# ScalarE copies and GpSimd sums in the post-attention chain, and expert tiles loaded six ahead

## The chip, the cores and the metric

The kernel runs on one core of a Trainium2 chip. A core has five engines that run their own instruction streams: TensorE (PE in the profile, with its weight loads as PEld), VectorE (DVE), ScalarE (ACT), GpSimd (POOL) and SyncE (SP, which here only issues DMA transfers). Matrix products land in PSUM, a small memory of eight banks of 128 partitions by 512 float32 numbers; everything else is kept in SBUF. The metric is device microseconds from the start to the end of one execution of the program; lower is better.

## The reference

The input x has 2 sequences of 2048 tokens with 256 features. All is float32, and every layernorm uses eps 1e-5.

1. Attention with 16 heads of 16 features: `qkv = x @ qkv_w + qkv_b`, a rotation of q and k (its angle depends on the head), scores divided by 4, softmax over all 2048 keys, the sum of values, `@ out_w + out_b`.
2. `x = layernorm(x + attention)`.
3. `n = layernorm(x) * g1 + be1`, then `x2 = x + n + n @ mix_w + mix_b`.
4. A mixture of 8 experts on `n2 = layernorm(x2) * g2 + be2`: router probabilities `softmax(n2 @ router_w)`, the best two experts of each token with those probabilities as weights (not normalised again), each expert `silu(n2 @ w1 + b1) @ w2 + b2` with 1024 hidden features, the weighted sum added to x2.
5. `out = layernorm(x + that)`, where x is the result of step 2.

## The kernel before, in words

**Attention.** The work is cut into 8 blocks of 512 query rows (4 per sequence). For each block there are four visits, one per group of four heads, so 32 visits in all; a visit walks over the 2048 keys in 16 chunks of 128. One chunk of one visit is a step, and there are 512 steps. A step of visit w does this:

- scores of 4 heads (L545), corrected by the row maxima through a second small product (L554), into four PSUM banks; ScalarE turns each into exponentials (L560, four instructions of 128x512);
- the value product of the step before (L575), which accumulates the unnormalised output in one PSUM bank; the values carry a column of ones, so that the sum of exponentials comes out as one more row;
- row maxima for a later visit, 18 steps ahead: four products (L501), two at a time, each into a bank of its own, and VectorE's maximum over each (L509, four reduces of 128x512). When a visit's maxima are complete, VectorE makes them ready (L519, L525, L528).

PSUM has three banks (`ps_mx`) for the row-maxima products and for everything that is done on the side. Two of them take the products of a half step; `bank(...)` takes one for each extra.

**The chain of a block.** Work on the side is entered by `later(k, f)`, to be done k steps later, and is handed out between the pieces of the steps, in an order that the program writes out by hand for TensorE, ScalarE, VectorE and SyncE. GpSimd's order is left to a scheduler. After a visit's last step ScalarE copies its output out of PSUM (L590). One step later `divide` transposes it (L597), VectorE takes the reciprocal of the sums (L600) and multiplies (L601) into `otok`. With a block's third group the input rows are fetched and GpSimd adds a bias row to them (`residual`, L660). With its fourth group the chain starts: `block` transposes the output (ScalarE empties the bank, L623), then `project` multiplies by `out_w`, in two halves of 256 rows. `two_products` does one half: eight matmuls into one bank (L636) and VectorE's addition to the residual (L643), then the moments of two groups of 128 rows, one per step (L647, L648). `norms` takes the layernorm's factors (L707, L708, and the square root by Newton steps in L137 to L146), with ScalarE and GpSimd applying them (L716, L730, L727). The second product, `mix`, uses `two_products` again. `lists` then takes another layernorm (L772), `logits` the router's product, `choose` the best two experts (L849 to L874), `places` the position of each row in its expert's list (L891 to L908), and GpSimd scatters the rows into the lists in HBM (L912).

The chain of a block runs during the next block's visits, one chain at a time. A block lasts 64 steps. The last two blocks of the 8 have a shorter time to finish in: the last one has its own pace (`pitch`, `gap`) and VectorE in place of GpSimd for the small operations. The projections to q, k and v of the second sequence are also done on the side, during the first blocks.

**Experts.** The lists are cut into 46 tiles, 25 whole ones of 256 rows and 21 half ones of 128. Each tile loads its rows (`xg`, L1239), the expert's `w1` and `w2` (1 MB each, L1252 and L1253), and its biases, all on SyncE's queue. Before, the loads are entered four tiles ahead: tiles 0 and 1 have their own two weight buffers in one pool, the others share four in another. TensorE transposes a tile's rows (L1269, emptied by VectorE, L1273), does the hidden product (L1298, then silu on ScalarE, L1307), and, one tile later, the second product (L1315). VectorE adds the bias and multiplies by the router's weight (L1325, L1326); GpSimd issues a DMA that adds the rows to `acc` in HBM (L1327, the scatter). These scatters, 71 in all, run in order.

**The end.** `acc` is read back in 8 parts, and each part is normalised (L1376 to L1385) and stored.

The functions that the change touches, and what calls them:

Of the kernel before, what the change touches and what calls it, by code (L numbers as in the profile page):

```python
# [32 lines left out]
P = 128  # L33
# [30 lines left out]
def seq_postln_kernel(  # L64
# [88 lines left out]
    with ExitStack() as actx:  # L153
# [431 lines left out]
        def attn_out(w):  # L585

            b, qb, g = visits[w]
            av = av_of.pop(w)
            avs = bp.tile([P, 512], F32, name="avs", tag="avs", bufs=2)
            nc.scalar.copy(avs, av)  # L590
            if g == 0:
                otok[b, qb] = bp.tile([P, 4, D], F32, name=f"otok_{b}_{qb}", tag="otok", bufs=1)

            def divide():
                ps = bank("ps_o", 4, P)
                for i in range(4):
                    nc.tensor.transpose(ps[:, i, :], avs[:, i * P : (i + 1) * P], ident)  # L597
                psv = ps.rearrange("p i (h c) -> p i h c", c=32)
                rd = bp.tile([P, 4, 4], F32, name="rd", tag="rd", bufs=2)
                nc.vector.reciprocal(rd, psv[:, :, :, HD])  # L600
                nc.vector.tensor_tensor(  # L601
                    otok[b, qb][:, :, g * 64 : (g + 1) * 64].rearrange(
                        "p i (h d) -> p i h d", d=HD
                    ),
                    psv[:, :, :, 0:HD],
                    rd.unsqueeze(3).to_broadcast([P, 4, 4, HD]),
                    ALU.mult,
                )
                if g == G - 2:
                    residual(b, qb)  # L610
                if g == G - 1:
                    later(1, lambda: holding("chain", block, b, qb))

            later(1, divide, 0.5, urgent=True)
# [15 lines left out]
        def two_products(name, turned_in, w, k, sum_, mv):  # L630
# [12 lines left out]
            nc.vector.tensor_add(sum_[:, 2 * k : 2 * k + 2, :], sum_[:, 2 * k : 2 * k + 2, :], ps)  # L643
# [6 lines left out]
            for i in range(2):  # L650
                later(1 + i, lambda i=i: moments(2 * k + i))
# [12 lines left out]
        def block(b, qb):  # L664
# [22 lines left out]
            def project(k):  # L687
                two_products("ps_p", oT, ow, k, xr, mv)
                if k == 1:
                    later(3, lambda: norms(n, xr, mv, eng, pitch, gap))  # L690
# [4 lines left out]
        def norms(n, xr, mv, eng, pitch, gap):  # L695
# [61 lines left out]
            def mix(k):  # L757

                two_products("ps_mix", nT, mixw, k, x2, mv2)
                if k == 1:  # L760
                    later(3, lambda: lists(n, xr, x2, mv2, eng, gap))
# [459 lines left out]
    first_tile = (0, NEARLY, NWHOLE)  # L1221

    def load_tile(t):
# [8 lines left out]
        pool, bufs = (wtp, 2) if t < 2 else (kp, 4)  # L1232
        b1 = kp.tile([P, NFC], F32, name=f"b1_{t}", tag="b1", bufs=5) if t >= 2 else wtp.tile(
            [P, NFC], F32, name=f"b1_{t}", tag="b1", bufs=2
        )
        w1t = pool.tile([P, 2, F], F32, name=f"w1_{t}", tag="w1", bufs=bufs)
        w2t = pool.tile([P, NFC, D], F32, name=f"w2_{t}", tag="w2", bufs=bufs)
        xg = wtp.tile([P, ns, D + 2], F32, name=f"xg_{t}", tag="xg", bufs=6)
# [16 lines left out]
        def load_b2():  # L1255
            b2t = kp.tile([P, D], F32, name=f"b2_{t}", tag="b2", bufs=6)
            nc.sync.dma_start(out=b2t, in_=b2[bass.ds(e, 1)].to_broadcast([P, D]))
            return b2t
# [78 lines left out]
    with tc.manual_schedule(engines=IN_ORDER):  # L1337
        DEPTH = 4
# [21 lines left out]
    for n in range(NTB):  # L1360

        o = (
            kp.tile([P, 4, D], F32, name=f"o_{n}", tag="o", bufs=NTB - 2)
            if n >= 2
            else wtp.tile([P, 2, F], F32, name=f"o_{n}", tag="w1", bufs=2)[:, 0, :].rearrange(
                "p (i d) -> p i d", i=4
            )
        )
        nc.sync.dma_start(out=o, in_=of[n])  # L1369
        os_.append(o)  # L1370
# [102 lines left out]
```

## Time and profile before

| | us |
|---|---|
| median of 3 runs | 2277.39 |
| lowest and highest of them | 2276.5, 2279.97 |
| the profiled execution | 2287.95 |
| its span | 2286.2 |
| busy: TensorE | 2209.9 (97%) |
| busy: VectorE | 1540.7 (67%) |
| busy: ScalarE | 1368.0 (60%) |
| busy: GpSimd | 471.3 (21%) |
| L509, row maxima on VectorE, 2048 reduces | 1274.2 |
| L560, exponentials on ScalarE, 2048 | 1057.6 |

The median is taken over runs without a profile, and the profiled execution is a run of its own, 10.56 us above it. All views of the trace are of that execution, and times in them count from the start of its span. A group row reads: line, engine, operation, written tile <- read tiles, shapes, how many, then busy time and the mean duration of one in ns, then the idle time of the engine just before them and what ended it. A timeline row reads: start and duration in us, engine, line, operation; in brackets the idle time before it and what ended that. A busy TensorE is not TensorE at its peak: a matmul that is held in the pipeline counts as busy. The granted clock of TensorE in this execution was 0.991 of full speed.

### The profile page before, as it was taken

How to read it: one execution, taken by the hardware profiler on the slowest of the kernel's cores; microseconds unless marked ns; L12 is line 12 of the kernel's file. 1: busy time of each engine (PE TensorE's matmuls, PEld its weight loads, DVE VectorE, ACT ScalarE, POOL GpSimd, SP SyncE). 2: the span in 40 equal slices, each digit the busy share in tenths (PEclk: the TensorE clock that was granted, in tenths of full speed). 3: DMA queues.
4: the chain of work that ended last, by engine and by line, in shares of the span. 5: the costliest groups of instructions: out<-in, count | busy, mean ns of one | idle time of the engine just before them, and what ended most of it. 6: DMA issues, size and time to landing. Idle time of an engine off the chain costs nothing. (4 is left out here: it accounts for less than half of the span.)

```text
span 2286.2 us, 39759 instructions
## 1 busy us (share of the span) xinstructions
PE 2209.9 (97%) x14192; PEld 1319.6 (58%) x14192; DVE 1540.7 (67%) x3108; ACT 1368.0 (60%) x2724; POOL 471.3 (21%) x826
## 2 busy tenths in 40 slices
PE   9999999999999999999999999999999999999992
PEld 4444555545555555555555555545548888889982
DVE  7887788788878888888888888888825211112213
ACT  2577667677767776677777667777774222222323
POOL 3112201231131112021111202112122322222113
PEclk9999999999999999999999999999999999999996
DMA  7635322221131111221111222111036677668995
GB/s 237 209 111 159 123 83 87 99 96 56 56 130 66 47 65 66 80 79 49 64 47 65 67 81 76 47 66 56 10 117 207 194 203 200 195 194 241 294 310 191
DMA packets 176117, 275.64 MB, mean 121 GB/s; under 512 B 22000, under 2 KB 107760, under 8 KB 175920
## 3 DMA queue, kind: packets, MB, share of 16 engines
q1 hardware_dynamic: 154960, 231.69, 30.8%
q0 software_dynamic: 20544, 40.59, 6.8%
q8 instruction: 112, 1.84, 0.3%
q14 instruction: 85, 0.70, 0.1%
q10 hardware_dynamic: 416, 0.83, 0.1%
HBM read 211.89 MB, written 62.74 MB: 120 GB/s over the span
## 5 line engine op out<-in xcount | busy, mean ns | idle before, releaser
L509 DVE TENSOR_REDUCE pm<-ps_mx 128x1 f32<-128x512 f32 x2048 | 1274.2, 683 | 191.1 <-PE ps_mx L501 181.9
L560 ACT ACTIVATE ex<-ps_sc 128x512 f32<-128x512 f32 x2048 | 1057.6, 603 | 355.2 <-PE ps_sc L554 332.8
L501 PE MATMUL ps_mx<-km,qm 64*128 64x512 f32 x2048 | 566.7, 469 | 19.3 <-DVE pm L509 17.9
L575 PE MATMUL av<-ex,vt 128*32 128x512 f32 x4096 | 546.2, 605 | 0.0
L501 PEld LDWEIGHTS ps_mx<-km,qm 64*128 64x128 f32 x2048 | 282.0, 183 | 452.3 <-DVE pm L509 340.3
L545 PE MATMUL ps_sc<-qm,km 64*128 64x512 f32 x2048 | 421.8, 394 | 0.0
L554 PE MATMUL ps_sc<-mrow,sel 64*128 64x512 f32 x2048 | 419.8, 393 | 0.7 <-ACT mrow L535 0.5
L1307 ACT ACTIVATE hT<-ps_h,b 128x256 f32<-128x256 f32 (+1 forms) x368 | 143.4, 426 | 365.4 <-PE ps_h L1298 277.3
L1298 PE MATMUL ps_h<-xT,w 128*128 128x256 f32 (+1 forms) x1472 | 258.5, 332 | 4.8 <-ACT hT L1307 2.7
L1315 PE MATMUL ps_y<-w,hT 128*128 128x256 f32 x1136 | 253.9, 379 | 2.1 <-DVE y L1325 2.1
L1298 PEld LDWEIGHTS ps_h<-xT,w 128*128 128x128 f32 x1472 | 222.0, 190 | 36.9 <-ACT hT L1307 7.9
L554 PEld LDWEIGHTS ps_sc<-mrow,sel 64*128 64x128 f32 x2048 | 204.2, 184 | 52.5 <-ACT mrow L535 9.6
L1315 PEld LDWEIGHTS ps_y<-w,hT 128*128 128x128 f32 x1136 | 212.0, 190 | 29.3 <-DVE y L1325 2.5
L545 PEld LDWEIGHTS ps_sc<-qm,km 64*128 64x128 f32 x2048 | 204.6, 185 | 37.2 <-ACT ex L560 15.4
L1273 DVE TENSOR_SCALAR xT<-ps_x,cols_sb 128x256 f32<-128x256 f32 (+1 forms) x92 | 40.1, 478 | 236.1 <-PE ps_x L1269 233.1
L1327 POOL DMA_INDIRECT acc<-y,xg x71 | 110.3, 1553 | 368.7 <-DVE y L1326 148.5
L575 PEld LDWEIGHTS av<-ex,vt 128*32 128x32 f32 x4096 | 80.9, 108 | 129.6 <-issue 122.3
L1325 DVE TENSOR_TENSOR y<-ps_y,b 128x256 f32<-128x256 f32 x71 | 30.1, 424 | 176.2 <-PE ps_y L1315 176.0
L132 POOL TENSOR_SCALAR op_mul<-mv 128x4 f32<-128x4 f32 x18 | 4.2, 234 | 438.1 <-DVE mv L648 437.1
L912 POOL DMA_INDIRECT x_list<-zx,at_i x64 | 63.9, 998 | 17.1 <-issue 13.6
L373 PE MATMUL ps_qk<-xT,wqk 128*128 128x512 f32 x128 | 65.3, 621 | 1.4 <-ACT xT L357 1.4
L391 POOL TENSOR_TENSOR full<-full,hi 128x512 f32<-128x512 f32 x27 | 34.4, 1274 | 154.7 <-DVE hi L387 140.6
(206 smaller groups left out, 1104.8 us busy)
## 6 DMA issues: line engine op xcount, KB each, us to landing
w<-in_w SPq DMA_DIRECT2D x92, 1024.0 KB
km<-st SPq DMA_DIRECT2D x248, 256.0 KB
qm<-st SPq DMA_DIRECT2D x62, 256.0 KB
st<-hi POOLq DMA_DIRECT2D x38, 256.0 KB
st<-full POOLq DMA_DIRECT2D x38, 256.0 KB
xg<-x_list SPq DMA_DIRECT2D x25, 258.0 KB
b<-in_b SPq DMA_DIRECT2D x46, 128.0 KB
st<-hi SPq DMA_DIRECT2D x18, 256.0 KB
```

The costliest lines, as they stand in the source:

```text
L373: nc.tensor.matmul(ps, lhsT=wqk[:, s, c, 8 * hh : 8 * hh + 8, :].rearrange("p h d -> p (h d)"), rhs=xT[b, tb][:, c, :], start=(c == 0), st ...
L501: nc.tensor.matmul(ps[j], lhsT=qm[w][pair][r, qt * P : (qt + 1) * P], rhs=km[w][pair][r, kb * 512 : (kb + 1) * 512], start=True, stop=True,)
L509: nc.vector.tensor_reduce(pm[w][:, qt, 2 * pair + j, kb : kb + 1], ps[j], AX.X, ALU.max)
L545: nc.tensor.matmul(sc[j], lhsT=km[w][pair][r, kt * P : (kt + 1) * P], rhs=qm[w][pair][r, :], start=True, stop=False,)
L554: nc.tensor.matmul(sc[j], lhsT=sel[pair][r, :], rhs=mrow[w][r, :], start=False, stop=True)
L560: nc.scalar.activation(ex, sc[j], AF.Exp, scale=0.25)
L575: nc.tensor.matmul(av[32 * h : 32 * h + 32, :], lhsT=vt[b][:, kt, at : at + 32], rhs=exs[h], start=(kt == 0), stop=(kt == 15),)
L912: ins = nc.gpsimd.indirect_dma_start(out=x_list, out_offset=bass.IndirectOffsetOnAxis(ap=at_i[:, k, i : i + 1], axis=0), in_=zx[:, k, i, : ...
L1298: nc.tensor.matmul(ps[:, j, :], lhsT=w1t[:, c, k * P : (k + 1) * P], rhs=xT[:, c, :], start=(c == 0), stop=(c == 1),)
L1307: nc.scalar.activation(hT[:, k, :], ps[:, j, :], AF.Silu, bias=b1[:, k : k + 1])
L1315: nc.tensor.matmul(ps, lhsT=hT[:, k, s * P : (s + 1) * P], rhs=w2t[:, k, :], start=(k == 0), stop=(k == NFC - 1),)
L1327: nc.gpsimd.indirect_dma_start(out=acc, out_offset=bass.IndirectOffsetOnAxis(ap=xg[:, s, D : D + 1].bitcast(I32), axis=0), in_=y, in_offse ...
```

## The change

There are two parts.

In the attention's chain, for the first six blocks, `divide` no longer lets VectorE read the transposed output in PSUM. ScalarE copies it to a buffer `od` in SBUF; one step later VectorE takes the reciprocal from there and GpSimd does the multiplication. `two_products` likewise has ScalarE copy the product to a buffer `pd`, and GpSimd add it to the running sum. `od` and `pd` share one buffer (tag "od", one copy of it). With that the block starts three steps after its last division rather than one, the moments come two and three steps after a product rather than one and two, and `norms` and `lists` four rather than three. The last two blocks keep the former form.

In the experts' stage the loads are entered six tiles ahead instead of four. The two weight buffers of the first pool become part of a ring of six, and the buffers of the rows (`xg`), `b1` and `b2` are increased to match. The final stage takes its eight buffers from the weights' places instead of having six of its own.

```diff
--- before.py
+++ after.py
@@ -591,25 +591,36 @@
             if g == 0:
                 otok[b, qb] = bp.tile([P, 4, D], F32, name=f"otok_{b}_{qb}", tag="otok", bufs=1)
 
+
+            last = b * TPB + qb >= NTB - 2
+
             def divide():
                 ps = bank("ps_o", 4, P)
                 for i in range(4):
                     nc.tensor.transpose(ps[:, i, :], avs[:, i * P : (i + 1) * P], ident)
-                psv = ps.rearrange("p i (h c) -> p i h c", c=32)
+                if last:
+                    divided(ps, nc.vector)
+                    return
+                od = ap_.tile([P, 4, P], F32, name="od", tag="od", bufs=1)
+                nc.scalar.copy(od, ps)
+                later(1, lambda: divided(od, nc.gpsimd), urgent=True)
+
+            def divided(o, eng):
+                ov_ = o.rearrange("p i (h c) -> p i h c", c=32)
                 rd = bp.tile([P, 4, 4], F32, name="rd", tag="rd", bufs=2)
-                nc.vector.reciprocal(rd, psv[:, :, :, HD])
-                nc.vector.tensor_tensor(
+                nc.vector.reciprocal(rd, ov_[:, :, :, HD])
+                eng.tensor_tensor(
                     otok[b, qb][:, :, g * 64 : (g + 1) * 64].rearrange(
                         "p i (h d) -> p i h d", d=HD
                     ),
-                    psv[:, :, :, 0:HD],
+                    ov_[:, :, :, 0:HD],
                     rd.unsqueeze(3).to_broadcast([P, 4, 4, HD]),
                     ALU.mult,
                 )
                 if g == G - 2:
                     residual(b, qb)
                 if g == G - 1:
-                    later(1, lambda: holding("chain", block, b, qb))
+                    later(1 if last else 3, lambda: holding("chain", block, b, qb))
 
             later(1, divide, 0.5, urgent=True)
 
@@ -627,7 +638,7 @@
         def small(name, *shape):
             return bp.tile([P, *shape], F32, name=name, tag=name, bufs=1)
 
-        def two_products(name, turned_in, w, k, sum_, mv):
+        def two_products(name, turned_in, w, k, sum_, mv, last):
 
             ps = bank(name, 2, D)
             for i in range(2):
@@ -640,7 +651,13 @@
                         start=(c == 0),
                         stop=(c == 1),
                     )
-            nc.vector.tensor_add(sum_[:, 2 * k : 2 * k + 2, :], sum_[:, 2 * k : 2 * k + 2, :], ps)
+            part = sum_[:, 2 * k : 2 * k + 2, :]
+            if last:
+                nc.vector.tensor_add(part, part, ps)
+            else:
+                pd = ap_.tile([P, 2, D], F32, name="pd", tag="od", bufs=1)
+                nc.scalar.copy(pd, ps)
+                nc.gpsimd.tensor_add(part, part, pd)
 
             def moments(i):
                 st = bp.tile([P, 6], F32, name="st", tag="st", bufs=3)
@@ -648,7 +665,7 @@
                 nc.vector.bn_aggr(mv[:, i, :], st)
 
             for i in range(2):
-                later(1 + i, lambda i=i: moments(2 * k + i))
+                later((1 if last else 2) + i, lambda i=i: moments(2 * k + i))
 
         xres: dict = {}
 
@@ -685,9 +702,9 @@
             mv = small("mv1", 4, 2)
 
             def project(k):
-                two_products("ps_p", oT, ow, k, xr, mv)
+                two_products("ps_p", oT, ow, k, xr, mv, n >= NTB - 2)
                 if k == 1:
-                    later(3, lambda: norms(n, xr, mv, eng, pitch, gap))
+                    later(3 if n >= NTB - 2 else 4, lambda: norms(n, xr, mv, eng, pitch, gap))
 
             for k in range(2):
                 later(3 + 2 * pitch * k, lambda k=k: project(k), 2.0)
@@ -756,9 +773,10 @@
 
             def mix(k):
 
-                two_products("ps_mix", nT, mixw, k, x2, mv2)
+                last = n >= NTB - 2
+                two_products("ps_mix", nT, mixw, k, x2, mv2, last)
                 if k == 1:
-                    later(3, lambda: lists(n, xr, x2, mv2, eng, gap))
+                    later(3 if last else 4, lambda: lists(n, xr, x2, mv2, eng, gap))
 
             normalize()
 
@@ -1219,6 +1237,7 @@
     b1v = cols[:, COL_B1:].rearrange("p (e k) -> e p k", e=E)
 
     first_tile = (0, NEARLY, NWHOLE)
+    DEPTH = 6
 
     def load_tile(t):
         k = sum(t >= first for first in first_tile) - 1
@@ -1229,13 +1248,12 @@
         at = nc.sync.value_load(
             start_i[0:1, i : i + 1], min_val=0, max_val=LIST // (ns * P) - 1
         )
-        pool, bufs = (wtp, 2) if t < 2 else (kp, 4)
-        b1 = kp.tile([P, NFC], F32, name=f"b1_{t}", tag="b1", bufs=5) if t >= 2 else wtp.tile(
-            [P, NFC], F32, name=f"b1_{t}", tag="b1", bufs=2
-        )
+
+        pool, bufs = (wtp, 2) if t % DEPTH < 2 else (kp, DEPTH - 2)
+        b1 = wtp.tile([P, NFC], F32, name=f"b1_{t}", tag="b1", bufs=DEPTH + 2)
         w1t = pool.tile([P, 2, F], F32, name=f"w1_{t}", tag="w1", bufs=bufs)
         w2t = pool.tile([P, NFC, D], F32, name=f"w2_{t}", tag="w2", bufs=bufs)
-        xg = wtp.tile([P, ns, D + 2], F32, name=f"xg_{t}", tag="xg", bufs=6)
+        xg = wtp.tile([P, ns, D + 2], F32, name=f"xg_{t}", tag="xg", bufs=DEPTH + 3)
         ins = nc.sync.dma_start(
             out=xg, in_=x_tiles[ns - 1][bass.ds(at, 1)].rearrange("a p s w -> (a p) s w")
         ).ins
@@ -1253,7 +1271,7 @@
         nc.sync.dma_start(out=w2t, in_=w2v[bass.ds(e, 1)].rearrange("a p k d -> (a p) k d"))
 
         def load_b2():
-            b2t = kp.tile([P, D], F32, name=f"b2_{t}", tag="b2", bufs=6)
+            b2t = kp.tile([P, D], F32, name=f"b2_{t}", tag="b2", bufs=DEPTH + 2)
             nc.sync.dma_start(out=b2t, in_=b2[bass.ds(e, 1)].to_broadcast([P, D]))
             return b2t
 
@@ -1335,7 +1353,6 @@
             )
 
     with tc.manual_schedule(engines=IN_ORDER):
-        DEPTH = 4
         loads = {t: load_tile(t) for t in range(2)}
         xT_of = {0: turn_tile(0, loads[0][0])}
         for t in range(2):
@@ -1359,13 +1376,10 @@
     os_ = []
     for n in range(NTB):
 
-        o = (
-            kp.tile([P, 4, D], F32, name=f"o_{n}", tag="o", bufs=NTB - 2)
-            if n >= 2
-            else wtp.tile([P, 2, F], F32, name=f"o_{n}", tag="w1", bufs=2)[:, 0, :].rearrange(
-                "p (i d) -> p i d", i=4
-            )
-        )
+        pool, bufs = (wtp, 2) if n < 2 else (kp, DEPTH - 2)
+        tag, k = ("w1", 2) if n < DEPTH else ("w2", NFC)
+        o = pool.tile([P, k, 2 * F // k], F32, name=f"o_{n}", tag=tag, bufs=bufs)
+        o = o.rearrange("p k f -> p (k f)")[:, 0 : 4 * D].rearrange("p (i d) -> p i d", i=4)
         nc.sync.dma_start(out=o, in_=of[n])
         os_.append(o)
     for n, o in enumerate(os_):
```

Line numbers after the change: the sum on VectorE L643 becomes L656, the copy `pd` is L659 and GpSimd's sum L660; the copy `od` is L605, the reciprocal L611 and the multiplication L612.

## The prediction

> **What bounds the kernel now.** I read the page first, then the list of waits, then VectorE's and TensorE's timelines of one attention stretch, then the expert stage in a table of windows, its TensorE and GpSimd timelines, and the chain that ended last. The page:
>
> ```profile
> span 2286.2 us, 39759 instructions
> PE 2209.9 (97%) x14192; PEld 1319.6 (58%) x14192; DVE 1540.7 (67%) x3108; ACT 1368.0 (60%) x2724; POOL 471.3 (21%) x826
> L509 DVE TENSOR_REDUCE pm<-ps_mx 128x1 f32<-128x512 f32 x2048 | 1274.2, 683 | 191.1 <-PE ps_mx L501 181.9
> ```
>
> TensorE looks full, but its busy time includes matmuls held up in the array. The list of waits says by whom:
>
> ```profile
> PEld ps_mx L501 <- DVE pm L509: 340.3, 512, 1.7
> ```
>
> The row-maxima products of the next attention visit (L501) write banks that VectorE must first reduce (L509). VectorE does four reduces per step:
>
> ```profile
> 954.86 0.69 DVE L643 TENSOR_TENSOR xr<-xr,ps_p 128x512 f32<-128x512 f32 x1 [1.72 <-PE ps_p L636]
> 955.46 2.48 DVE L509 TENSOR_REDUCE pm<-ps_mx 128x1 f32<-128x512 f32 x4
> 957.86 0.42 DVE L647 BATCH_NORM_STATS2 st<-xr 128x6 f32<-128x256 f32 x1
> 958.31 0.18 DVE L648 BATCH_NORM_AGGREGATE mv<-st 128x2 f32<-128x6 f32 x1
> 958.41 2.45 DVE L509 TENSOR_REDUCE pm<-ps_mx 128x1 f32<-128x512 f32 x4
> ```
>
> TensorE's step without extras lasts 2.705 us (score group to score group) against 2.48 us of reduces: 0.22 us to spare. When moments (L647, L648: 0.57 us) fall into it, a row-maxima pair swells:
>
> ```profile
> 948.68 0.52 PE L501 MATMUL ps_mx<-km,qm 64*128 64x512 f32 x2
> ...
> 958.89 0.73 PE L501 MATMUL ps_mx<-km,qm 64*128 64x512 f32 x2
> ```
>
> So a VectorE extra costs about its length less 0.33, while a step with a product of its own on TensorE (+1.92 us) hides it. Over the 64 steps of a block (898.8 to 1098.9 us) the excess over this pace is 8.7 us, 7.4 of it beside VectorE extras. Steps whose extra is emptied by ScalarE (the turned tiles, L623 and L625) lose 0.00 to 0.01.
>
> The expert stage is bound otherwise. Its 25 whole tiles run at TensorE's pace (windows: PE 100 of 100 us from 1990 to 2090, DMA share 0.68). In the 21 half tiles the weights' DMA is full; columns after the length are PE, PEld, DVE, ACT, POOL, clock, DMA share, GB/s:
>
> ```profile
> 2159.00:2180.00 21.00, 21.00 (x147) 19.81 (x147) 4.12 (x12) 6.24 (x23) 4.64 (x3) 1.00 1.00 306
> 2202.00:2224.00 22.00, 18.13 (x121) 16.37 (x120) 3.74 (x10) 6.35 (x23) 4.64 (x3) 1.00 0.91 282
> ```
>
> Near the end TensorE waits for loads, and the scatters on GpSimd's queue (L1327), which the chain ends on, trail:
>
> ```profile
> 2212.36 0.44 PE L1269 MATMUL ps_x<-ident,xg 128*128 128x128 f32 x2 [1.84 <-DMA xg<-x_list]
> 2222.09 0.44 PE L1269 MATMUL ps_x<-ident,xg 128*128 128x128 f32 x2 [1.16 <-DMA xg<-x_list]
> ```
> ```profile
> 2202.26 1.55 POOL L1327 DMA_INDIRECT acc<-y,xg  x1 [7.76 <-issue]
> 2210.17 1.55 POOL L1327 DMA_INDIRECT acc<-y,xg  x1 [6.36 <-issue]
> ...
> 2246.84 1.55 POOL L1327 DMA_INDIRECT acc<-y,xg  x1 [2.87 <-issue]
> 2251.40 1.55 POOL L1327 DMA_INDIRECT acc<-y,xg  x1 [3.01 <-issue]
> ```
>
> **The sum's frame.** The profiled execution took 2287.95 us (span 2286.2, 1.75 around it), 10.56 above the median 2277.39; I subtract gains from the one and give the same difference on the other.
>
> **Part 1, divisions and products of the first six blocks.** Leaving VectorE: 24 multiplies (L601, 0.42) and 24 sums (L643, 0.69), 26.7 us. The 24 reciprocals (0.26) stay, a step later. Arriving: 48 ScalarE copies of 128x512 out of PSUM, 0.59 to 0.62 by L535 and L590, 29 us; and on GpSimd 24 multiplies of 128x256 and 24 sums of 128x512.
> - ScalarE: a step's four exponentials take 2.41 us (L560, 603 ns). The copies fall into steps that TensorE's transposes (+0.58) or products (+1.92) lengthen to 3.28 and 4.62, so 3.02 fits. Queued behind a copy are exponentials, and TensorE's value products behind those; the turned tiles, of the same length, lost nothing. Cost 0.
> - GpSimd: the sum is L391's shape, 1.27. The multiply has no row: half of L391 and a quarter of L727 (2.38) give 0.6, L730 (128x256, 1.23) is above it; I take 0.72, nearest the tensor-tensor rows. In all 24×0.72 + 24×1.27 = 48 us on an engine 21% busy. Behind them queue the chain's small operations, the residual sum (L660, which waits for its DMA) and the scatters. The residual sum, entered at step 33, ran at 34 to 35; if GpSimd's order puts it ahead of a product's sum, that sum still starts some 3.4 us before the next copy into the single buffer, which product and division share. The chain gives each result one more step: three steps to the block, two to the moments. Cost 0, unless they hold VectorE (below).
> - What VectorE keeps in one block, by the program's order after. Before (898.8 to 1098.9): row maxima's end at 62 to 0 .54; multiply at 2 .21; moments 6 to 8 .66; 12, 13 .38; 14 to 16 (maxima's end, moments, norms) 1.37; 18 .19; 26 to 28 .66; 30 to 35 1.54; 46 to 50 (choice of experts) 1.81: 7.36. After: 62 to 0 .54; moments 10, 11 .42; 14's maxima hidden by the product moved to 14, then .15 and moments .21 (16, 17); 18 (reciprocal and five norm operations, 0.87 less 0.33, a trailing .04) .58; 30 to 33 .75; moments 37, 38 .42; lists 39 .24; 46 to 48 .38; the choice at 52 and 53 .67 and 1.09: 5.45. So 1.9 per regular block, three of them: 5.7.
> - Blocks beside the second batch's projections lose 3.1 and 2.3 more at steps 49 to 51, where the choice meets division and projections; the chain now reaches these after the division. I take 2.6 each, 5.2. The last changed block, whose neighbour's divisions stay, gives 1.3, the first period (divisions alone) 0.4. Sum 12.6.
> - Holds. One small VectorE operation with its operands in SBUF was held until a GpSimd sum ended:
>
> ```profile
> 400.95 0.95 DVE L772 TENSOR_SCALAR v<-mv 128x4 f32<-128x4 f32 x1
> ```
> ```profile
> 399.49 2.38 POOL L660 TENSOR_TENSOR xr<-xr,wide_rows 128x1024 f32<-128x1024 f32 x1 [5.26 <-DMA xr<-in_x]
> ```
>
> It takes 0.16 elsewhere; here it ended at 401.90, as the sum did (401.87). Reduces out of PSUM are not held:
>
> ```profile
> 1019.36 2.38 POOL L787 TENSOR_TENSOR xr<-xr,x 128x1024 f32<-128x1024 f32 x1 [27.53 <-DVE x L643]
> ```
> ```profile
> 1019.13 2.48 DVE L509 TENSOR_REDUCE pm<-ps_mx 128x1 f32<-128x512 f32 x4
> ```
>
> In the new order GpSimd's multiply meets the norms' small operations at step 18, and a sum meets the end of the row maxima at 30: about 0.6 a block, between 0 and 1.7 (two multiplies at 0.72 less what is idle, and a sum at 1.27 less 0.33). Six blocks: 3.6 (0 to 10). Attention: 12.6 − 3.6 = 9; bounds 2 and 16 (all twelve moment steps free as well).
>
> [...]
>
> **Part 2, six tiles ahead.** The weights ring grows from four buffers to six, so two more half tiles are in flight. One is 2.36 MB, 7.8 us at 302 GB/s (2090 to 2187), against TensorE's 7.245 per tile. While whole tiles run the DMA has room (0.68 to 0.70), so at the first half tile the loads stand two tiles, 15.6 us, further on, and the full stretch ends near 2216, not 2231. TensorE's stalls between 2187 and 2224 (0.49, 0.43, 1.84, 0.87, 1.16 and slower pieces: 6.0) go. Scatters come 8.4 us apart while the DMA is full (14 from 2092.28 to 2210.17), 4.4 apart afterwards. The last then comes at 2216 + 6.3×4.41 = 2244 rather than 2251.4: 7.6. I take 7, between TensorE's 6.0 and the scatters' 7.6 (bounds 0 and 8.5). The reading of sums, last norms and stores behind it (31 us) is the same. SP issues the same loads in the same order, each only released earlier. The first weights still wait for the attention's end, as their place was the attention's; the two rings' b1, b2 and row buffers cost nothing.
>
> Sum: 9 + 7 = 16, so 2272 of the profiled execution, 2261 of the median.
>
> **Rivals.**
> - No holds: 12.6 + 7.6 = 20.2, 2257. For it: GpSimd's 48 operations lie mostly beside reduces. Against: the row at 400.95.
> - Attention gives nothing: the holds eat it (9 more than the 3.6 taken), or the sums' and moments' new steps cost what the old ones did, the moved steps colliding elsewhere. Then 2270, by the loads alone. Against: the 0.00 of the rows that ScalarE empties.
> - The tail doesn't move: scatters stay 8.4 apart, or the loads fill the DMA in any order. Then 2268. Against: the 4.4 spacing as soon as loads end.
> - Slower: GpSimd's new operations hold VectorE for their length each. 48 us against the 19.6 of both gains: it decides from 0.41 us per operation; in full it gives 2277 + 28 = 2305, at 0.6 us per operation 2287. For it: the row at 400.95. Against: the row maxima at 1019.13, and that VectorE's time is mostly those.
>
> **How the numbers follow.** Likeliest, both gains and some holds: .5 (2257 to 2266). No holds .17; loads alone .11; attention alone .11; slower .11, of which .09 beyond 0.2% (4.6 us, about what a measurement tells from no change); .03 of the two that give one gain alone fall within it. The range reaches from 2254 (the bounds 16 and 7.6) to 2271, leaving out the slower rival and a tenth of the rest. Faster .86, same .05, slower .09.
>
> **What would show it.** Reduce rows unchanged at about 620 ns when not waiting; the wait of L501 on L509 down from 340 by some 30 or more; no row-maxima swelling at the division and product steps; copies near 0.6 us in longer steps without TensorE waiting for exponentials. Rows of small VectorE operations above 0.3 us would count the holds. In the half tiles no load wait before the tiles' transposes, and a last scatter near 2235 to 2245 on the new clock's zero, 7 earlier against the attention's end. The prediction fails if GpSimd's order puts a long wait (the residual's DMA, the scatters) ahead of a multiply, so that ScalarE's copy waits for its buffer and exponentials with it, or if the scatters don't follow the DMA share.

## The result, and the profile after

The changed kernel takes 2267.64 us (median of 7 runs) against 2275.11 us of the kernel before (7 runs): the ratio is 0.9958, 95% interval 0.9944 to 0.9972, some 9.6 us faster (the ratio comes from the runs, not from the two medians, which differ by 7.5 us). One of the seven executions of the changed kernel took 7045.77 us and is left out of the ratio; the other six took 2262.99 to 2269.59. The range of 2254 to 2271 held the median; the point, 2261, was 6.6 us too low, and of the 16 us forecast 9.6 came.

The profiled execution took 2262.99 us. Its page, with the lines that answer to those of before:

```profile
span 2261.3 us, 39849 instructions
PE 2199.6 (97%) x14192; PEld 1320.4 (58%) x14192; DVE 1517.0 (67%) x3060; ACT 1394.7 (62%) x2772; POOL 518.1 (23%) x874
L509 DVE TENSOR_REDUCE pm<-ps_mx 128x1 f32<-128x512 f32 x2048 | 1274.5, 682 | 250.4 <-PE ps_mx L501 246.5
```

VectorE lost 23.7 us of work, ScalarE gained 26.7 and GpSimd 46.8; VectorE idles 250 us before the row maxima instead of 191. The list of waits on TensorE's weight loads has fewer waits on the reduces, 466 instead of 512, the longest 1.1 us instead of 1.7:

```profile
PEld ps_mx L501 <- DVE pm L509: 324.9, 466, 1.1
```

The new instructions by groups (ScalarE's copies, then GpSimd's multiplication and one of the two kinds of sum):

```profile
L605 ACT COPY od<-ps_o 128x512 f32<-128x512 f32 x24 | 14.1, 587 | 11.0 <-PE ps_o L600 11.0
L659 ACT COPY pd<-ps_p 128x512 f32<-128x512 f32 x12 | 7.0, 587 | 20.3 <-PE ps_p L647 20.3
...
L612 POOL TENSOR_TENSOR otok<-od,rd 128x256 f32<-128x256 f32 x24 | 14.9, 620 | 189.7 <-DVE rd L611 176.3 <-DVE v L725 13.3
L660 POOL TENSOR_TENSOR xr<-xr,pd 128x512 f32<-128x512 f32 x12 | 15.4, 1281 | 217.6 <-ACT pd L659 217.6
```

A copy takes 587 ns, a multiplication 0.62 us (0.72 was assumed), a sum 1.28.

What no line of the prediction foresaw stands where the attention ends and the experts' stage begins, on TensorE's timeline:

```profile
1685.86 2.85 PE L575 MATMUL av<-ex,vt 128*32 128x512 f32 x16
1691.56 0.63 PE L1287 MATMUL ps_x<-ident,xg 128*128 128x128 f32 x4 [2.86 <-DMA xg<-x_list]
1695.49 2.04 PE L1316 MATMUL ps_h<-xT,w 128*128 128x256 f32 x4 [3.30 <-DMA w<-in_w]
```

TensorE waits 2.86 us for the first tile's rows and 3.30 us for its weights. Before, the same place looked like this:

```profile
1705.52 2.51 PE L575 MATMUL av<-ex,vt 128*32 128x512 f32 x16
1708.71 0.66 PE L1269 MATMUL ps_x<-ident,xg 128*128 128x128 f32 x4 [0.68 <-ACT avs L590]
1710.06 1.15 PE L1298 MATMUL ps_h<-xT,w 128*128 128x256 f32 x4 [0.69 <-DVE xT L1273]
```

From the attention's last product to the first hidden product it was 2.03 us, now it is 6.78. Four matmuls take 2.04 us instead of 1.15: the clock has fallen to half (column "clock", 0.50). In a table of windows (columns: length, PE, PEld, DVE, ACT, POOL, clock, DMA share, GB/s):

```profile
1684.00:1694.00 10.00, 5.33 (x36) 1.88 (x28) 0.99 (x2) 3.80 (x8) 0.00 (x0) 1.00 0.37 115
1694.00:1700.00 6.00, 4.51 (x13) 3.61 (x14) 0.68 (x2) 1.76 (x2) 0.00 (x0) 0.50 1.06 372
```

The list of waits says what SyncE, which issues the loads, stood before:

```profile
SPq L1257 <- PE av L575: 12.4, 1, 12.4
```

It waited 12.4 us for the attention's last product and issued the first tile's load at 1688.74 us, when the attention was over. Before, that load was issued at 1694.71 us, 13.3 us before the attention's end at 1708.03. SyncE's timelines, before and after:

```profile
1694.71 0.41 SPq L1239 DMA_DIRECT2D xg<-x_list  x1
```
```profile
1688.74 0.41 SPq L1257 DMA_DIRECT2D xg<-x_list  x1
```

The difference of the two profiled executions, 25 us, is not the effect. The first profile of the kernel before is of an execution with stalls that others of it lack (below); I take effects from the ratios (in the experiments both kernels ran on the same chip), and use a second profile of the kernel before beside the first.

### The profile page after: what moved, and what is told of

It reads as the page before. It is cut to its first block, busy times and chain, and to the rows that moved or that the text cites. A ratio compares the mean times of both kernels' runs of the same rounds, so it can differ in the third digit from the quotient of the medians.

```text
span 2261.3 us, 39849 instructions
## 1 busy us (share of the span) xinstructions
PE 2199.6 (97%) x14192; PEld 1320.4 (58%) x14192; DVE 1517.0 (67%) x3060; ACT 1394.7 (62%) x2772; POOL 518.1 (23%) x874
## 4 chain that ended last, share of the span: by engine, by line
PE 91%; DVE 6%; ACT 1%; DMA 1%; issue 1%; POOL 0%; SPq 0%; ACTq 0%; POOLq 0%; DVEq 0%
PE av L575 21%; PE ps_mx L501 18%; PE ps_h L1316 11%; PE ps_y L1333 10%; PE ps_sc L554 10%; PE ps_sc L545 10%; DVE pm L509 3%; PE ps_qk L373 3%; PE ps_v L445 1%; PE ps_p L647 1%; PE ps_mix L647 1%; PE ps_o L600 1%; PE ps_m L533 1%; PE ps_l L833 1%; PE ps_x L1287 1%
## 5 line engine op out<-in xcount | busy, mean ns | idle before, releaser
L509 DVE TENSOR_REDUCE pm<-ps_mx 128x1 f32<-128x512 f32 x2048 | 1274.5, 682 | 250.4 <-PE ps_mx L501 246.5
L501 PE MATMUL ps_mx<-km,qm 64*128 64x512 f32 x2048 | 557.3, 468 | 11.5 <-DVE pm L509 10.3
L501 PEld LDWEIGHTS ps_mx<-km,qm 64*128 64x128 f32 x2048 | 282.0, 183 | 434.0 <-DVE pm L509 324.9
L554 PEld LDWEIGHTS ps_sc<-mrow,sel 64*128 64x128 f32 x2048 | 203.9, 184 | 53.1 <-ACT mrow L535 10.5
L930 POOL DMA_INDIRECT x_list<-zx,at_i x64 | 64.1, 1001 | 17.1 <-issue 13.3
L660 POOL TENSOR_TENSOR xr<-xr,pd 128x512 f32<-128x512 f32 x12 | 15.4, 1281 | 217.6 <-ACT pd L659 217.6
```

What stands on the lines that cost most here:

```text
L501: nc.tensor.matmul(ps[j], lhsT=qm[w][pair][r, qt * P : (qt + 1) * P], rhs=km[w][pair][r, kb * 512 : (kb + 1) * 512], start=True, stop=True,)
L509: nc.vector.tensor_reduce(pm[w][:, qt, 2 * pair + j, kb : kb + 1], ps[j], AX.X, ALU.max)
L554: nc.tensor.matmul(sc[j], lhsT=sel[pair][r, :], rhs=mrow[w][r, :], start=False, stop=True)
L930: ins = nc.gpsimd.indirect_dma_start(out=x_list, out_offset=bass.IndirectOffsetOnAxis(ap=at_i[:, k, i : i + 1], axis=0), in_=zx[:, k, i, : ...
```

## The experiments

**The two parts alone.** `chain_only` keeps the part of ScalarE and GpSimd and takes the experts' stage from the kernel before; `loads_only` is the opposite. The edits are the two halves of the diff.

> The chain's part alone (ScalarE's copies, GpSimd's multiplications and sums), the experts' loads four tiles ahead as before. Theory: the attention ends some 9 us earlier (a regular block loses 5.9 us beside VectorE's extras instead of 7.4), the experts' first tiles are loaded during the attention as before, so 2265 to 2267, ratio 0.996. Rival (the chain gives half of that, the loads the other half of the changed kernel's gain): 2270, ratio 0.998.

Measured: 2265.72 us, ratio 0.9950 (0.9933 to 0.9966), 11.4 us. The profile's attention ends at 1691.3 us, 9.9 us before that of the second profile of the kernel before (1701.2). The rival's 0.998 is excluded.

> The loads' part alone, the chain as before. Theory: the last scatter comes some 7 us earlier against the start of the experts' stage, but the first tile's loads are issued only when the attention's last product has ended (13 us later than before), TensorE stands idle for 5 us more, its clock halves for some microseconds, 8 to 13 us in all; so no gain, 2275 to 2281, ratio 1.000 to 1.003. Rival (the first loads' wait costs nothing that counts): 2268 to 2270, ratio 0.997 to 0.998.

Measured: 2275.18 us, ratio 0.9991 (0.9981 to 1.0001); the first hidden product comes 6.6 us after the attention. The loads' part by itself gives next to nothing, as the theory had it, if a little better. The rival's 0.997 to 0.998 is excluded.

**The wait of the first loads.** Tiles are allocated in pools that lie behind each other in SBUF. Before, the first pool of the experts' stage (weights and rows of the first tiles, `xT`) ended at byte 111680 of a partition, and the attention's pool began at 115552. The nine row buffers and eight b1 buffers of the changed kernel push its end to 118112, over the attention's two buffers for the maxima (`mt`). The first load into the pool then carries waits on all that the attention's pool does: TensorE, VectorE and the queues of its DMAs. `free_first` moves `xT` (4096 bytes) to the second pool, so that the first ends at 114016:

```diff
-        xT = wtp.tile([P, 2, ns * P], F32, name=f"xT_{t}", tag="xgT", bufs=2)
+        xT = kp.tile([P, 2, ns * P], F32, name=f"xT_{t}", tag="xgT", bufs=2)
```

> The changed kernel with the tiles' turned rows (xT) allocated in the second pool instead of the first, so that the first pool no longer reaches into the bytes of the attention's pool. Theory: the first tile's loads are issued at the last scatter into the lists, before the attention's end; first hidden product 2 us after the attention's last product instead of 6.8, no dip of the clock there; 2258 to 2261, ratio 0.993 to 0.994. Rival (the wait of the first loads is not what eats the gain): as the changed kernel, 2266 to 2268, ratio 0.996.

Measured: 2258.68 us, ratio 0.9915 (0.9899 to 0.9931). TensorE's and SyncE's timelines:

```profile
1688.50 2.84 PE L575 MATMUL av<-ex,vt 128*32 128x512 f32 x16
1692.02 0.66 PE L1287 MATMUL ps_x<-ident,xg 128*128 128x128 f32 x4 [0.68 <-ACT avs L590]
1693.37 1.15 PE L1316 MATMUL ps_h<-xT,w 128*128 128x256 f32 x4 [0.70 <-DVE xT L1291]
```
```profile
1678.90 0.41 SPq L1257 DMA_DIRECT2D xg<-x_list  x1
```

The first load is issued 12.4 us before the attention's end at 1691.34, the gap is 2.03 us again, and there is no half clock there. The address of `xT` is the same as before the move; only the pool it counts to, and with it the wait, has changed. Between the two comparisons the wait cost 0.9958 − 0.9915 = 0.0043, 9.8 us: half of what the two parts give without it. In the profiles the time from the attention's last product to the end of the span falls from 572.6 us in the changed kernel to 566.0, by 6.6.

The same move on the loads' part alone:

> The loads' part alone, with xT in the second pool as in free_first, so that the first tile's loads don't wait for the attention's end. Theory (two gains that add up, and one loss in the loads' part): loads_only gave 0.9991, the freed first loads give 0.0043 more as between the changed kernel and free_first, so 0.9948 to 0.9968, 2267 to 2272. Rival (the loads' part gives nothing, free_first is the chain's gain alone): 2277, ratio 0.999 to 1.000.

Measured: 2268.63 us, ratio 0.9963 (0.9947 to 0.9978), and the chain's 0.9950 times 0.9963 is 0.9913, `free_first`'s 0.9915. The parts add up. The wait cost 0.0028 here, 6.4 us; behind the attention the two profiles take 572.2 us (`loads_only`) and 565.8, again 6.4 apart.

To have the wait without the rest, `wait_alone` gives the kernel before eight row buffers instead of six, which moves the first pool's end to 115840 (and puts the final stage's buffers into the weights' places, to make room):

```diff
-        xg = wtp.tile([P, ns, D + 2], F32, name=f"xg_{t}", tag="xg", bufs=6)
+        xg = wtp.tile([P, ns, D + 2], F32, name=f"xg_{t}", tag="xg", bufs=8)
```

> The kernel before with eight buffers of tile rows (xg) instead of six, so that the first pool reaches into the attention's pool; the final stage's buffers lie in the weights' places, as in the changed kernel, to make room. Chain and four tiles ahead stay. Theory (the first loads' wait is the loss): first hidden product 6.6 to 6.8 us after the attention's last product instead of 2.0, a dip of the clock there, 6 to 10 us slower than before: 2282 to 2286, ratio 1.002 to 1.004. Rival (the loss between the changed kernel and free_first came from xT's pool or from six tiles): as before, ratio 0.999 to 1.000.

Measured: 2288.04 us against 2287.17, ratio 1.0002 (0.9987 to 1.0016). The gap and the half clock are there (7.3 us, 6.8 us of half clock), the loss is not: the expectation was wrong. Either the wait is hidden later, or the two buffers pay it back. Two kernels tell this apart. `pad_alone` has the wait and no more buffers, `rows8_free` the buffers and no wait (both have the final stage's buffers in the weights' places as well):

```diff
+    wtp.tile([P, 1040], F32, name="pad", tag="pad", bufs=1)
```
```diff
-        xg = wtp.tile([P, ns, D + 2], F32, name=f"xg_{t}", tag="xg", bufs=6)
+        xg = wtp.tile([P, ns, D + 2], F32, name=f"xg_{t}", tag="xg", bufs=8)
...
-        xT = wtp.tile([P, 2, ns * P], F32, name=f"xT_{t}", tag="xgT", bufs=2)
+        xT = kp.tile([P, 2, ns * P], F32, name=f"xT_{t}", tag="xgT", bufs=2)
```

> The kernel before with a tile of 4160 bytes that nothing uses in the first pool, so that the pool reaches into the attention's bytes; the final stage's buffers in the weights' places to make room; nothing else. wait_alone had the same wait and two more row buffers, and came out as before. Theory (the wait costs, and the row buffers paid it back there): first hidden product 6.6 to 7.4 us after the attention's last product, a dip of 6.8 us of half clock, 5 to 9 us slower, ratio 1.002 to 1.004. Rival (the wait is hidden further on, by loads that catch up): 0.999 to 1.001.

> The kernel before with the eight row buffers of wait_alone, but xT in the second pool, so that the first loads don't wait; four weight buffers in the ring as before. Theory (row buffers alone let the loads run further ahead, since SyncE waited 96 us for scatters to free one): 4 to 7 us faster, ratio 0.997 to 0.998, most of what six tiles ahead gives (0.9963). Rival (row buffers give nothing, the weights' ring is what counts): 0.9995 to 1.0005.

Measured: `pad_alone` 2290.88 us, ratio 1.0024 (1.0012 to 1.0036), gap 7.9 us with 6.8 us of half clock; `rows8_free` 2280.27 us, ratio 0.9977 (0.9966 to 0.9988), gap 2.04 us. Their product is 1.0001, `wait_alone`'s 1.0002. So the wait costs 5.5 us in the kernel before, and two row buffers alone give 5.2 us. The final stage's new places, which all three have, cost nothing that shows: from the last scatter to the end it takes 35.0 to 35.2 us in these three, and 34.8 and 36.0 in the two profiles of the kernel before. That two row buffers give 5.2 us is a result on the loads' part as well. The waits of SyncE, before and in `rows8_free`:

```profile
SPq L1253 <- PE ps_y L1315: 209.1, 26, 26.2
SPq L1239 <- DMA acc<-y,xg: 96.3, 25, 13.3
```
```profile
SPq L1253 <- PE ps_y L1315: 282.2, 39, 26.1
```

Before, the row load (L1239) waited 25 times for a scatter that still held a row buffer, and the weight loads that SyncE issues behind it waited too: the longest of these waits, 13.3 us, ended with the row load at 1751.45 us, and that tile's first weight load (L1252) followed at 1752.64. With eight buffers that line is gone and the weights' ring is the limit that is left. Of the 0.0037 of the loads' part, 0.0023 come from buffers of 2 KB, and 0.0014 are left for the two pairs of weight buffers that join the ring and the ninth row buffer; the intervals of the two ratios, from different comparisons, overlap.

**Whether it is VectorE's time or ScalarE's emptying of the bank.** `copies_only` is `free_first` with VectorE, not GpSimd, doing the multiplication and the sum from ScalarE's copies:

```diff
-                later(1, lambda: divided(od, nc.gpsimd), urgent=True)
+                later(1, lambda: divided(od, nc.vector), urgent=True)
...
-                nc.gpsimd.tensor_add(part, part, pd)
+                later(1, lambda: nc.vector.tensor_add(part, part, pd))
```

> As free_first, with ScalarE's copies kept, but VectorE doing the multiplications and sums from the copies instead of GpSimd. Theory (the gain comes from VectorE's time): each sum of 0.69 and each reciprocal with multiplication of about 0.66 falls into a step without cover and costs 0.33 to 0.36; four of each in a block, less the hold of 0.45, gives 2.3 more per block, 14 in six: 2270 to 2274. Rival (it is the bank that ScalarE empties sooner): 2259 as free_first.

Measured: 2276.27 us, ratio 0.9996 (0.9986 to 1.0007): as slow as before, 18.5 us (0.0081) worse than `free_first`. The loads' part, worth 0.9963 without its wait, is in this kernel too, so the chain with ScalarE's copies and VectorE's arithmetic is by itself some 0.003 slower than the chain before. The bank emptied by ScalarE gives nothing without VectorE's time. The 4 us above the 14 expected have at least in part a reason in the profile: in five of the six blocks VectorE's multiplication falls beside a GpSimd sum and takes 1.65 to 2.45 us. One of them:

```profile
1029.83 1.65 DVE L612 TENSOR_TENSOR otok<-od,rd 128x256 f32<-128x256 f32 x1
```
```profile
1028.81 2.38 POOL L677 TENSOR_TENSOR xr<-xr,wide_rows 128x1024 f32<-128x1024 f32 x1 [22.59 <-DMA xr<-in_x]
```

It takes 1.65 us instead of 0.42 and ends at 1031.48, after GpSimd's sum (1031.19); that step loses 1.52 us.

**The hold by GpSimd in the changed kernel.** In the profile after, VectorE's and GpSimd's timelines at a block's norms:

```profile
964.99 0.24 DVE L611 RECIPROCAL rd<-od 128x16 f32<-128x16 f32 x1
...
965.35 0.61 DVE L137 TENSOR_SCALAR q<-v 128x8 int32<-128x8 int32 x1
966.00 0.17 DVE L140 TENSOR_SCALAR r<-q 128x8 int32<-128x8 int32 x1
```
```profile
965.31 0.62 POOL L612 TENSOR_TENSOR otok<-od,rd 128x256 f32<-128x256 f32 x1 [2.66 <-DVE v L725]
```

The shift (L137) ends at 965.96, GpSimd's multiplication at 965.93. In the step in question TensorE loses 0.85 us. It is so in five of the six changed blocks. `late_multiply` meant to part them by entering the multiplication two steps later:

```diff
+                if g == 1 and not last:
+                    rd = reciprocal(o)
+                    later(2, lambda: multiplied(o, rd, eng), urgent=True)
```

> As free_first, with GpSimd's multiplication of a block's second visit two steps later, so that it is not running when VectorE begins the norms' small operations. If GpSimd's operation holds VectorE's, the first shift (L137) falls from 0.61 to 0.17 us, that step's loss from 0.85 to about 0.40, and the attention ends 6 x 0.45 = 2.7 us before that of free_first. If the five small operations cost that by themselves, it stays.

Measured: 2259.12 us, ratio 0.9915, L137 still 0.61 us. It told nothing of the hold: GpSimd's instructions are not bound to the steps, and the multiplication ran at the same moment, as soon as the reciprocal was there (0.08 us behind its end, 0.09 in `free_first`). `norms_later` moves VectorE's side instead:

```diff
-                    later(3 if n >= NTB - 2 else 4, lambda: norms(n, xr, mv, eng, pitch, gap))
+                    later(3 if n >= NTB - 2 else 5, lambda: norms(n, xr, mv, eng, pitch, gap))
```

> As free_first, with the norms of the first six blocks one step later (five steps after the second product instead of four), so that VectorE's five small operations come after GpSimd's multiplication has ended. In late_multiply the multiplication ran at the same place as before, so that it told nothing of the hold. If the operation of GpSimd holds VectorE's: the first shift (L137) 0.17 us instead of 0.61, the loss of that step 0.45 to 0.55 instead of 0.85, 2 us in the six blocks; the later steps of the chain shift too and may give or take 2 us; 2255 to 2258. If the small operations cost this by themselves: L137 stays at 0.61, 2259.

Measured: 2252.4 us, ratio 0.9894 (0.9874 to 0.9913), better than both kernels, and by 0.0021 than `free_first`, where the intervals overlap and the chip was another. The profiles show it without that doubt: from the first step to the last product the attention takes 1604.9 us, against 1610.5 in the changed kernel, with no half clock in either. The timelines:

```profile
960.77 0.24 DVE L611 RECIPROCAL rd<-od 128x16 f32<-128x16 f32 x1
...
963.73 0.17 DVE L137 TENSOR_SCALAR q<-v 128x8 int32<-128x8 int32 x1
```
```profile
961.09 0.62 POOL L612 TENSOR_TENSOR otok<-od,rd 128x256 f32<-128x256 f32 x1 [2.66 <-DVE rd L611]
```

L137 takes 0.17 us and the norms cost 0.30 in place of 0.85. The gain in all is more than this: a block loses 5.0 us instead of 5.9, because the second product (`mix`) now shares its step with the end of the row maxima, which came one step behind it, and hides it. The two blocks beside the second sequence's projections become 1.6 us shorter each (210.2 and 208.7 us instead of 211.8 and 210.3), and the last changed block 0.4 us longer. The choice of experts no longer meets a projection there, but that is not the reason: its first step loses 0.68 us either way (5.31 us where a projection's step takes 4.63, 3.38 where a plain one takes 2.70). What else shortens these two blocks stays open, and none of this was tried one by one.

**The profiles.** `before_again` is the kernel before, for a second profile.

> The kernel before once more, for a second profile. Its first profile had eight stretches of 1.0 to 1.4 us in the attention in which TensorE stood still beside no operation of another engine (484, 697 to 701, 895, 1089 to 1095, 1295, 1496 us and one at 1461), which no profile of the changed kernels has. If they belong to that execution alone, this profile has none and a span some 8 to 10 us shorter; if the former order of the chain causes them, they come back at the same steps.

Measured: a span of 2273.9 us and none of the stalls. `after_again` is the changed kernel.

> The changed kernel once more on the chip of the experiments, for a ratio next to theirs and a second profile. Theory: 0.9945 to 0.996 as before, 2265 to 2269; the runs whose mean clock is 0.988 rather than 0.992 have a longer stretch at half clock where the experts' stage starts. Rival: in those runs the half clock lies elsewhere, in the attention.

Measured: 2277.12 us against 2287.17, ratio 0.9961 (0.9946 to 0.9975), clock 0.989 in the profile; the ratio is the earlier one again although both kernels are some 10 us slower on that chip, which the expected time had not allowed for. Ahead of the end, where TensorE has nothing left to do, its half clock lies in four places: 6.8 us at the start of the experts' stage, as in the first profile of the changed kernel, and three times 3.4 us elsewhere, twice in the attention and once behind it. So the theory was wrong on the clock, as the stretch at the stage's start has not grown, and the rival was right in the main. The stalls of about 1.3 us are back as well, right behind the last scatter into the lists.

## Why the prediction was right, and where it was not

**The chain: right, and its size too.** 9 us were forecast (2 to 16); `chain_only` measures 11.4 (7.7 to 15.3). The loss of a step is what it takes above the pace of a step of its kind. In the attention's steps, the second profile of the kernel before against the profile after, the loss beside VectorE's extras falls from 2.7, 9.0, 8.2, 7.3, 7.3, 7.3, 7.4 us in the first seven stretches of 64 steps to 1.8, 6.4, 6.9, 6.0, 5.9, 5.9, 6.4: 9.9 us. The stretches as a whole are 11.0 us shorter.

| term | forecast | measured |
|---|---|---|
| three regular blocks, 1.9 less 0.6 each | 3.9 | 4.1 |
| two beside projections, 2.6 less 0.6 each | 4.0 | 3.9 |
| last changed block, 1.3 less 0.6 | 0.7 | 1.0 |
| first period | 0.4 | 0.9 |

- ScalarE's copies cost nothing: their steps lose 0.00 to 0.01 where no moments fall into them, as forecast from the turned tiles.
- The hold was there at one of the two places named, at the norms, with about 0.55 us for a block, in five of the six; the sum at the end of the row maxima (step 30) held nothing, the small operations there keep their 0.18 to 0.22 us. The 0.6 a block that was taken for both places was near it.
- The slower rival (each GpSimd operation holds VectorE for its length) needed 0.41 us for each of 48; five of the 48 held VectorE, for 0.44 us each on L137.
- One sign was sized wrongly: the wait of L501 on L509 was to fall from 340 by 30 or more. It fell from 340.3 (337.6 in the second profile) to 324.9, although the steps gained what was forecast.

The hold shows in new cases too: the multiplication of `copies_only`, which reads `od` and `rd` in SBUF, took 1.65 us under a GpSimd sum instead of 0.42, and the shift took 0.61 instead of 0.17 under GpSimd's multiplication. Moving the work to GpSimd paid in spite of it: on VectorE the same work gave 0.9996, on GpSimd 0.9915.

**The loads: right in size, on a reading that was partly of one execution.** 7 us were forecast; without the wait they give 0.0037, 8.4 us (5.0 to 12.1), and in the profiles 6.9 from the attention's end (572.7 us in `before_again`, 565.8 in `loads_free_first`). But the 6.0 us of TensorE's stalls between 2187 and 2224 us were mostly of the first profiled execution: from the first hidden product to TensorE's end it is 528.0 us in `before_again`, 534.5 in the first profile and 526.8 in `loads_free_first`, so TensorE gains 1.2 (and `chain_only`, with the former loads, takes 527.3). What goes is the scatters' lag: the last one is issued 6.6 us behind TensorE's end in `before_again` and 2.3 in `loads_free_first`, 4.3 less; the remaining 1.4 us of the 6.9 lie behind it (36.0 and 34.6 us to the end). The way it goes is the one forecast. In the two profiles, whose attentions end at 1701.2 and 1701.1 us, the scatters pass from some 8 us apart to 4.4 or 4.5 about 19 us apart, at 2220 in the first and 2201 in the second:

```profile
2212.11 1.55 POOL L1327 DMA_INDIRECT acc<-y,xg  x1 [6.26 <-DVE y L1325]
2220.18 1.55 POOL L1327 DMA_INDIRECT acc<-y,xg  x1 [6.52 <-issue]
2224.79 1.55 POOL L1327 DMA_INDIRECT acc<-y,xg  x1 [3.06 <-issue]
```
```profile
2201.04 1.55 POOL L1327 DMA_INDIRECT acc<-y,xg  x1 [6.63 <-DVE xT L1273]
2205.51 1.55 POOL L1327 DMA_INDIRECT acc<-y,xg  x1 [2.92 <-DVE y L1326]
```

In the changed kernel the scatters have caught up three tiles before the end, and the last lies 2.1 us behind:

```profile
2214.19 1.55 POOL L1345 DMA_INDIRECT acc<-y,xg  x1 [5.47 <-DVE y L1344]
2222.09 1.55 POOL L1345 DMA_INDIRECT acc<-y,xg  x1 [6.35 <-DVE y L1344]
2226.52 1.55 POOL L1345 DMA_INDIRECT acc<-y,xg  x1 [2.87 <-issue]
```

And the loads stand further ahead not by the weights' ring alone: the row buffers, taken as costing and giving nothing, give 0.0023 of the 0.0037 by themselves (`rows8_free`, with the intervals as wide as said above).

**The step that failed** is the sentence "The first weights still wait for the attention's end, as their place was the attention's; the two rings' b1, b2 and row buffers cost nothing." Only the tiles from the third on waited before; the loads of the first two were issued 13 and 10 us ahead of the attention's end, and SyncE's timeline of before showed it. The row buffers cost this head start, because they push the first pool's end into the attention's bytes. The term missing from the sum is 5.5 us (`pad_alone`), 6.4 (`loads_only`) or 9.8 (`free_first`), with intervals that overlap. With it in the sum, 16 less 5.5 to 9.8 is 6 to 10.5, and 9.6 came; with all three terms as measured, 11.4 + 8.4 − 9.8 is 10.0. That the wait is larger beside the chain's part than alone is not shown: behind the attention the profiles differ by 6.6 and 6.4 us. The time lay in the range in part by luck: the upper end, 2271, was drawn for holds, and for a tail that doesn't move, not for this wait.

## What to carry to other kernels

A larger ring of buffers can cost time far from where it is used: here the end of a pool moved from byte 111680 to 118112, into the bytes of an earlier stage, and the first load of the next stage waited for that stage's end. The profile showed it as one wait of the DMA queue on the last product, 12.4 us, and it cost 5.5 to 9.8 us. Look at addresses, or at that wait, whenever buffers are added, and count the small buffers of a ring as well as the large ones: here the row load waited 25 times for a buffer, for up to 13.3 us, with the loads behind it on the queue, and two more row buffers gave 5.2 us. Moving work from VectorE to ScalarE and GpSimd paid where VectorE's time was the wait (0.0050 here), and it paid more when GpSimd's multiplication didn't run beside VectorE's small SBUF operations (L137 0.17 us instead of 0.61): parting the two by one step, with what else that step moved, shortened the attention by another 5.6 us.

## What the runs showed of the hardware that was not expected

- All five executions whose first loads waited show TensorE's clock at half for 6.8 us at the start of the experts' stage (the changed kernel twice, `loads_only`, `wait_alone`, `pad_alone`), behind two gaps of TensorE of 2.8 to 3.0 and 3.1 to 4.3 us; none of those without the wait shows it there. Elsewhere the half clock comes in single stretches of 3.4 us, one to three in most executions; 6.8 us is twice that. In the attention the single ones cost about 1.4 us each (198.7 for 197.2 us in a block of `chain_only`).
- Of the 18 single stretches in the attentions of the 14 profiles, 17 have no gap of TensorE before them; they begin right behind a chain's router product (L815 before, L833 after: 16 matmuls of 128x8), during which the profile has TensorE busy for 1.9 us. The half clocks of an execution begin on a grid of 3.413 us (the two in the attention of `chain_only`, at 867.13 and 1263.08 us, are 116 times that apart). The 17 router products that ended 0.00 to 0.36 us before a point of this grid were followed by a half clock; the other 95 of the 14 profiles ended 0.44 us or more before the next point, and none of them was. So in these profiles the blocks that lost the 1.4 us are, but for one, those whose router product ended just before a point of the grid, and the clock halved although the profile calls TensorE busy during that product. The 18th, in `copies_only`, comes 3.4 us behind a gap of 1.5 us.
- Some executions have a stall of 0.8 to 1.3 us in most blocks, right behind the last scatter into the lists: at step 57 of a regular block in the first profile of the kernel before and in `wait_alone`, `pad_alone` and `rows8_free`, at step 62 in `after_again`, where the scatters end later. The kernel before has none in `before_again`, nor has `copies_only`, nor any of the first four experiments. TensorE's timeline of the first profile of the kernel before shows one inside a pair of row-maxima products:

```profile
1295.81 0.39 PE L501 MATMUL ps_mx<-km,qm 64*128 64x512 f32 x1
1297.08 0.49 PE L501 MATMUL ps_mx<-km,qm 64*128 64x512 f32 x1 [0.89 <-DVE pm L509]
```

TensorE is not what stands still first. The reduce that releases it ran from 1296.34 to 1297.03, although its product had ended at 1295.05, and ScalarE's next exponential started at 1296.48, although its scores were complete at 1295.51; no engine starts an operation between 1295.81 and 1296.34. GpSimd's last scatter had ended at 1295.35. The cause stays open. It means that two profiled executions can differ where the kernels don't: the attention of the kernel before takes 1629.8 us in its first profile (1.4 of them for a half clock) and 1621.4 in its second.
